# Setting the causal mask for the score maxima with GpSimd in SBUF, in place of mask products of TensorE, from the third batch on

## The chip, the core and the metric

The kernel runs on one core of a Trainium2 chip, in one launch. Five engines work side by side and wait for each other by semaphores: TensorE (in profiles PE for products and PEld for its weight loads), VectorE (DVE), ScalarE (ACT), GpSimd (POOL) and SyncE (SP, here for transfers). Each takes its instructions in the order in which the program has them. TensorE writes to PSUM; GpSimd works in SBUF. The metric is device time in microseconds (us) of one execution.

## The reference: what is computed

A block of a transformer on 8 sequences ("batches") of 256 tokens with 256 features: layer norm, attention with 32 query heads and 8 key heads of size 8, layer norm and residual, then a mixture of 8 experts (two are chosen per token) with shared experts beside them, layer norm and residual. The part that the change touches is the softmax of the attention:

```python
scores = jnp.einsum('bkgtd,bksd->bkgts', qg, k) / jnp.sqrt(jnp.asarray(hd, x.dtype))
causal = jnp.tril(jnp.ones((T, T), dtype=bool))
scores = jnp.where(causal[None, None, None, :, :], scores, jnp.asarray(-jnp.inf, x.dtype))
attn = jax.nn.softmax(scores, axis=-1)
ctx = jnp.einsum('bkgts,bksd->bkgtd', attn, v)
```

## The kernel before

**Two passes over the scores.** A batch's 256 queries are two tiles of 128 (`tt` or `t` is 0 or 1), and so are its keys. In a first pass (`maxima_of`, `maxima`, L448 to L490) TensorE forms scores with queries on the partitions, and VectorE takes each query's maximum over the keys (L484). The causal mask belongs into these scores, since a key that is not seen may not raise the maximum: on the diagonal tile a second product of TensorE (L477) adds -1e30 to what is masked, by an identity matrix times a mask in bf16. `split_shift` (L492) splits the negated maxima into two parts, `shiftT` (L499) transposes them on TensorE (`pm`), and SyncE's queue copies them as additional rows into the queries `qA` (L514). In the second pass (`weights_of`, L519) TensorE forms the scores again with keys on the partitions (`scT`, L522), now less their maxima by these rows; ScalarE takes the exponential (L530); on the diagonal tile GpSimd sets what is masked to zero in SBUF (L532). `values` (L543) multiplies by the values, into `av`; when a query tile is done, `av` is copied to `avs` (L559, by ScalarE for batches 0 and 1 and by VectorE from batch 2 on), and `softmaxed` (L562) transposes `avs` on TensorE into `pav` (L570) and divides (L574, L577).

The sweep of the first pass over a batch is cut into tiles of up to 512 columns[...]: 10 tiles for `tt` = 0 (8 of 3 key heads by 128 keys and 2 of 512 columns) and 16 tiles for `tt` = 1 (512 columns, with one or two products each), so 26 reductions, 32 score products and 32 mask products a batch. Of the mask products 8 have 384 columns, 16 have 256 and 8 have 128.

**Buffers.** Scores of both passes, the expert products `gu` and the down products `po` share five PSUM buffers (`ps_mm`, L113). Transposes, projections and the router's products share two (`ps_tp`, L114). The exponentials have nine buffers `ex` in SBUF (L1052).

**What else a batch does.** `norm1` and `normed1`, `transposed` (L324), `project` (L340: queries, keys and values, rotated by VectorE with `ra` and `rb`, summed to `full` by GpSimd, L372), `split` (L377: seven pieces a tile, each a copy and a subtraction on GpSimd, L396 and L397), `keysT` (L402, with copies `kA` by VectorE, L421 and L423), `queriesT` (L434, copies by ScalarE), the projection of the context and its norm (L610 on, `rstd` on GpSimd, L282 and L283), `residual` on GpSimd (L624), the router (`logits` L659, `first_choice` L686, `second_choice` L695, `places` L715, `shares` L708 with `den`), and `scatter` (L741): for each of two token tiles and each of two experts GpSimd multiplies a weight (L746) and issues an indirect transfer to `slots` (L752). Shared experts (`shared_gate_up` L800, `shared_down` L818) are spread between, with `th` on ScalarE (L812) and `th`, `sact` on VectorE (L813, L814).

**What sets the order.** Each step is entered by `at(when, step, ...)` (L297) with a time in units of a batch; the steps are sorted by it (L1192) and their instructions issued in that order, so that every engine's queue has them in this order. Batch b's first pass starts at b - 0.98 with 0.032 from tile to tile (L1089 to L1095), its second pass at b (L1098), its router at some b + 1.5 and its two scatters at b + 1.63 and b + 1.66 (L1140). So at any time the first pass of one batch, the second pass of the one before and the router of the one before that are in work. After the last batch come the experts' blocks (from L1195), which the change doesn't touch.

Of the kernel before, what the change touches and what calls it, by code (L numbers as in the profile page):

```python
# [10 lines left out]
F32 = mybir.dt.float32  # L11
F32R = mybir.dt.float32r
BF16 = mybir.dt.bfloat16
I32 = mybir.dt.int32
AF = mybir.ActivationFunctionType
ALU = mybir.AluOpType
# [3 lines left out]
P = 128  # L20
EPS = 1e-5
NEG = -1e30
HD = 8
HB = 32
SHIFT = 96
SQ = 32
EB = 256
# [3 lines left out]
def attn_moe_kernel(  # L31
# [46 lines left out]
    nc = tc.nc  # L78
    B, T, D = x.shape
# [10 lines left out]
    ISC = IS // P  # L90
    G = 4
    NKV = NH // G
    NK = NKV * HD
    NC = NKV // G
    J = 3
    NS = -(-NKV // J)
# [5 lines left out]
    RW = 4  # L102
# [23 lines left out]
    NREG = -(-NSLOT // (16 * EB)) * 16  # L126
# [84 lines left out]
    def set_up_router():  # L211
        nonlocal order, ones, before, upto, region0, fills, blocks, cum, unused

        order = const.tile([P, NSEL], F32, name="order")
        for e in range(NSEL):
            nc.gpsimd.memset(order[:, e : e + 1], float(NSEL - e))


        ones = const.tile([P, P], BF16, name="ones")
        before = const.tile([P, P], BF16, name="before")  # L220
        nc.gpsimd.memset(ones, 1.0)
        nc.gpsimd.affine_select(
            out=before,
            in_=ones,
            pattern=[[1, P]],
            compare_op=ALU.is_gt,
            fill=0.0,
            base=0,
            channel_multiplier=-1,
        )  # L230
        upto = const.tile([P, 2 * NSEL, 2 * NSEL], F32, name="upto")
        nc.gpsimd.memset(upto, 1.0)
        nc.gpsimd.affine_select(
            out=upto,
            in_=upto,
            pattern=[[1, 2 * NSEL], [-1, 2 * NSEL]],
            compare_op=ALU.is_ge,
            fill=0.0,
            base=0,
            channel_multiplier=0,  # L240
        )

        def counter(name, *pattern, base=0):
            sizes = [n for _, n in pattern]
            i = const.tile([P, *sizes], I32, name=f"{name}_i")
            nc.gpsimd.iota(i, pattern=[*map(list, pattern)], base=base, channel_multiplier=0)
            f = const.tile([P, *sizes], F32, name=name)
            nc.vector.tensor_copy(f, i)
            return f

        region0 = counter("region0", (NTOK, NSEL))

        fills = counter("fills", (-P, 2), (EB, NTOK // EB - 1), base=EB + P)
        blocks = counter("blocks", (1, NBLK - NSEL))
        cum = const.tile([P, NT + 1, NSEL], BF16, name="cum")
        nc.vector.memset(cum[:, 0, :], 0.0)


        unused = aconst.tile([NREG, EB, RW], I32, name="unused")
        nc.gpsimd.memset(unused, 0)  # L260
        nc.gpsimd.iota(
            unused[:, :, 1], pattern=[[1, EB]], base=NTOK, channel_multiplier=0
        )
        nc.gpsimd.memset(records, 0)
        nc.gpsimd.iota(
            records[:, :, :, 0], pattern=[[P, NT], [0, 2]], base=0, channel_multiplier=1
        )
        nc.gpsimd.iota(
            records[:, :, :, 1], pattern=[[1, NT], [0, 2]], base=0, channel_multiplier=NT
        )  # L270
# [26 lines left out]
    def at(when, step, *args):  # L297
        timeline.append((when, len(timeline), step, args))
# [100 lines left out]
    def heads_in(c):  # L399
        return min(J, NKV - c * J)  # L400
# [46 lines left out]

    def maxima_of(b, tt):  # L448

        width = (tt + 1) * P  # L450
        for c in range(NS):
            per = min(512 // width, heads_in(c))
            for k0 in range(0, heads_in(c), per):
                nk = min(per, heads_in(c) - k0)
                ng = 512 // (nk * width)
                for g0 in range(0, G, ng):
                    yield c, c * J + k0, nk, g0, ng

    def maxima(b, tt, c, k0, nk, g0, ng):

        qA, kst = qAs[b % 3], ksts[b % 3]
        if ("nmx", b, tt) not in held:
            held["nmx", b, tt] = small.tile(
                [P, NKV, G], F32, tag="nmx", name=f"nmx{b}_{tt}", bufs=2
            )
        nmx = held["nmx", b, tt]
        width = (tt + 1) * P
        sc = ps_mm.tile([P, ng, nk, width], F32, tag="mm", name="sc")
        for g in range(ng):
            nc.tensor.matmul(  # L470
                sc[:, g, :, :],
                lhsT=qA[0:SHIFT, c * G + g0 + g, ts(tt, P)],
                rhs=kst[0:SHIFT, k0 : k0 + nk, 0:width],
                start=True,
                stop=False,
            )
            nc.tensor.matmul(  # L477
                sc[:, g, :, width - P :],
                lhsT=ident_b,
                rhs=mask.unsqueeze(1).to_broadcast([P, nk, P]),  # L480
                start=False,
                stop=True,
            )
        nc.vector.tensor_reduce(  # L484
            nmx[:, k0 : k0 + nk, g0 : g0 + ng].rearrange("p k g -> p g k"),
            sc,
            AX.X,
            ALU.max,
            negate=True,
        )  # L490

    def split_shift(b, tt):  # L492
        nmx = held.pop(("nmx", b, tt))
        nhl = small.tile([P, NKV, 2, G], F32R, tag="nhl", name=f"nhl{b}_{tt}", bufs=2)
        nc.vector.tensor_copy(nhl[:, :, 1, :], nmx)
        nc.vector.tensor_tensor(nhl[:, :, 0, :], nmx, nhl[:, :, 1, :], ALU.subtract)
        held["nhl", b, tt] = nhl
# [551 lines left out]
        )  # L1049


    EX = 9  # L1052
    at(0.6, clear_slots)
    at(0.7, clear_sums)
    for i in range(PIECES):
# [18 lines left out]
    for b in range(B):  # L1074
        if b > 0:

            at(b - 2.08, norm1, b)
            at(b - 2.035, normed1, b)
            for tt in range(TT):
                a = b - 1.95 + 0.45 * tt  # L1080
                at(a, transposed, b, tt)
                at(a + 0.05, project, b, tt)
                for i in range(1 + 2 * NS):
                    at(a + 0.09 + 0.03 * i, split, b, tt, i)
                at(a + 0.22, keysT, b, tt)
                for c in range(NS):
                    at(a + 0.28 + 0.06 * c, queriesT, b, tt, c)
            at(b - 1.25, keys_apart, b)
        when = b - 0.98  # L1089
        for tt in range(TT):  # L1090
            for m in maxima_of(b, tt):
                at(when, maxima, b, tt, *m)
                when += 0.032
            at(when + 0.001, split_shift, b, tt)
            at(when + 0.07, shiftT, b, tt)  # L1095
        last = b == B - 1
        parts_of = [(c, t) for c in range(NC) for t in range(TT)]
        when, unit = b, 0.98 / (NC * 3 * G)  # L1098
        if b == 0:
            parts_of.sort(key=lambda part: part[1])  # L1100
            when, unit = -0.4, 0.04
        for c, t in parts_of:
            if b == 0 and t > 0:
                when = max(when, 0)
            for s in range(t + 1):
                for j in range(G):
                    at(when, weights_of, b, c * G + j, s, t)
                    when += unit
                at(when + 0.05, values, b, c, s, t)
            a = when + (0.1 if last else 0.12)  # L1110
            at(a, softmaxed, b, c, t)
            if c == NC - 1:
                at(a + 0.05, contextT, b, t)
                at(a + 0.09, projected, b, t)
        a = b + (1.175 if last else 1.24)
        at(a if last else a - 0.04, norm_y, b)
        at(a, normed_y, b)
        for t in range(TT):
            at(a + 0.02 + 0.01 * t, residual, b, t)
        at(a + 0.07, norm2, b)  # L1120
        at(a + (0.07 if last else 0.125), normed2, b)
        if last:
            for t in range(TT):
                at(a + 0.145 + 0.015 * t, tokensT, b, t)
            at(a + 0.175, logits, b)
            at(a + 0.1751, first_choice, b)
            at(a + 0.1752, second_choice, b)
            at(a + 0.225, places, b)
            at(a + 0.2251, shares, b)
            for t in range(TT):  # L1130
                at(a + 0.226, scatter, b, t)
            continue
        for t in range(TT):
            at(a + 0.19 + 0.02 * t, tokensT, b, t)
        at(a + 0.24, logits, b)
        at(a + 0.27, first_choice, b)
        at(a + 0.302, second_choice, b)
        at(a + 0.37, places, b)
        at(a + 0.375, shares, b)
        for t in range(TT):  # L1140
            at(a + 0.39 + 0.03 * t, scatter, b, t)
# [189 lines left out]
```

## Time and profile before

| | us |
|---|---|
| median of the runs (826.61 to 831.75) | 826.7 |
| the profiled execution: own time | 836.61 |
| the profiled execution: span, mean clock 0.962 | 834.9 |
| masks, L477: 256 products, recorded busy time | 74.6 |
| score products of the first pass, L470: 256 | 101.4 |
| reductions, L484: 208 | 129.3 |
| exponentials, L530: 192 | 113.6 |
| GpSimd's selects on the exponentials, L532: 128 | 81.3 |

The profile is of one execution, which had its own time; sums are made against that one. The page gives each engine's busy time, the same in 40 slices (a digit is tenths), the chain that ended last and the costliest groups; the trace answers for single stretches: busy times, waits ("who waited for whom") and the instructions in order of time, with start and duration. Recorded durations of TensorE's products overlap from one to the next. In the timeline lines the columns are start, duration, engine, line, operation, output and inputs, shapes, count, and in brackets the idle time before it with what ended it.

The attention takes the first 500 us, the experts' blocks the rest. The reductions of the first pass run from 92.8 to 134.6 us for batch 2, from 206.9 to 259.4 for batch 4, from 269.0 to 321.5 for batch 5, and end at 437.9 with batch 7.

### The profile page before, as it was taken

The page shows a single profiled execution, that of the slowest core. Times are in us where ns is not written, and L with a number is a line of the kernel's source. Part 1 is how long each engine was busy: PE and PEld are TensorE (multiplying, and loading weights), DVE is VectorE, ACT ScalarE, POOL GpSimd, SP SyncE. Part 2 cuts the span into 40 slices and gives each one's busy share as a digit, 9 for nine tenths or more (in the row PEclk, how much of TensorE's full clock was granted, in tenths as well). Part 3 has the DMA queues.
Part 4 walks back from the last instruction along what each step waited for, and adds up shares of the span by engine and source line. Part 5 has one row for each costly group of instructions (what it writes and reads, how often), then busy time and mean ns, then how long its engine had stood idle before and what let it go on. Part 6 is the DMA issues. An engine that isn't in the chain of part 4 may idle for free. (4 is left out here: it accounts for less than half of the span.)

```text
span 834.9 us, 11892 instructions
## 1 busy us (share of the span) xinstructions
PE 768.9 (92%) x3981; PEld 584.0 (70%) x3981; DVE 492.5 (59%) x1412; ACT 251.5 (30%) x552; POOL 345.2 (41%) x616
## 2 busy tenths in 40 slices
PE   5989899999999999999999996879999999999962
PEld 3545566766766767767666665768888888888951
DVE  5756677667677677676675546156564556532215
ACT  2554444234234244244234321011111111111203
POOL 4567455435435435435243422422222343452213
PEclk8799899999999999999999998889999999999986
DMA  5033200000000000000000005513646657578942
GB/s 152 4 85 88 87 16 16 7 22 15 7 22 15 7 21 15 8 22 15 21 8 3 20 6 202 171 40 121 213 138 186 212 160 226 174 216 302 312 117 101
DMA packets 31907, 74.62 MB, mean 89 GB/s; under 512 B 9136, under 2 KB 26032, under 8 KB 28896
## 3 DMA queue, kind: packets, MB, share of 16 engines
q1 hardware_dynamic: 20304, 58.17, 20.1%
q0 software_dynamic: 8224, 10.03, 6.2%
q10 hardware_dynamic: 3312, 5.60, 2.3%
q8 instruction: 34, 0.56, 0.3%
q14 instruction: 33, 0.27, 0.1%
HBM read 59.36 MB, written 11.80 MB: 85 GB/s over the span
## 5 line engine op out<-in xcount | busy, mean ns | idle before, releaser
L778 PE MATMUL gu<-xgT,w 128*128 128x256 f32 (+1 forms) x840 | 166.5, 358 | 6.1 <-ACT xgT L972 5.8
L778 PEld LDWEIGHTS gu<-xgT,w 128*128 128x128 f32 x840 | 146.2, 193 | 24.0 <-ACT xgT L972 6.1
L778 PE MATMUL gu<-x2T,ws_sb 128*128 128x256 f32 x640 | 156.5, 392 | 6.2 <-PEq L1232 6.1
L530 ACT ACTIVATE ex<-scT 128x512 f32<-128x512 f32 x192 | 113.6, 597 | 136.8 <-PE scT L522 123.3
L484 DVE TENSOR_REDUCE nmx<-sc 128x2 f32<-128x512 f32 (+2 forms) x208 | 129.3, 642 | 26.5 <-PE sc L477 26.2
L778 PEld LDWEIGHTS gu<-x2T,ws_sb 128*128 128x128 f32 x640 | 122.2, 197 | 28.7 <-issue 7.3
L532 POOL TENSOR_SCALAR_AFFINE_SELECT ex<-ex 128x512 f32<-128x512 f32 x128 | 81.3, 641 | 113.9 <-ACT ex L530 113.7
L1008 POOL DMA_INDIRECT sums<-yb,of x37 | 58.3, 1577 | 121.4 <-DVE yb L1007 81.3
L470 PE MATMUL sc<-kst,qA 96*128 96x512 f32 (+2 forms) x256 | 101.4, 427 | 0.7 <-issue 0.4
L522 PE MATMUL scT<-qA,kst 102*128 102x512 f32 x192 | 97.3, 515 | 1.8 <-DMA qA<-nm 1.8
L997 ACT ACTIVATE sg<-gu 128x256 f32<-128x256 f32 (+1 forms) x105 | 37.7, 359 | 196.4 <-PE gu L778 154.4
L985 DVE STREAM_TRANSPOSE xgT<-xg 32x128 f32<-32x128 f32 x240 | 72.6, 303 | 26.9 <-DMA xg<-rows,of 17.2
L791 PE MATMUL po<-w,act 128*128 128x256 f32 x370 | 83.1, 379 | 0.0
L791 PE MATMUL po<-ws_sb,sact 128*128 128x256 f32 x320 | 75.4, 393 | 5.6 <-DVE sact L814 4.2
L998 DVE TENSOR_TENSOR act<-sg,gu 128x256 f32<-128x256 f32 (+1 forms) x105 | 39.2, 387 | 63.6 <-ACT sg L997 58.7
L791 PEld LDWEIGHTS po<-w,act 128*128 128x128 f32 x370 | 69.8, 190 | 9.2
L791 PEld LDWEIGHTS po<-ws_sb,sact 128*128 128x128 f32 x320 | 61.8, 197 | 19.8 <-DVE sact L814 4.6
L477 PE MATMUL sc<-mask,ident_b 128*128 128x256 bf16 (+2 forms) x256 | 74.6, 294 | 0.0
L813 DVE SCALAR_TENSOR_TENSOR th<-th,gu 128x256 f32<-128x256 f32 x70 | 29.3, 418 | 66.3 <-ACT th L812 63.1
L926 POOL DMA_INDIRECT xg<-rows,of x39 | 37.8, 970 | 62.3 <-DMA of<-slots 29.9
L470 PEld LDWEIGHTS sc<-kst,qA 96*128 96x128 f32 x256 | 51.6, 202 | 13.6 <-issue 3.8
L550 PE MATMUL av<-ex,v_aug 128*32 128x512 f32 x384 | 58.2, 605 | 1.3 <-POOL ex L532 1.3
(167 smaller groups left out, 848.2 us busy)
## 6 DMA issues: line engine op xcount, KB each, us to landing
w<-in_routed SPq DMA_DIRECT2D x23, 1920.0 KB
ws_sb<-in_shared ACTq DMA_DIRECT2D x8, 480.0 KB
xs<-in_x SPq DMA_DIRECT2D x8, 256.0 KB
rows<-x2n SPq DMA_DIRECT2D x8, 256.0 KB
acc<-sums SPq DMA_DIRECT2D x4, 512.0 KB
sums<-ya SPq DMA_DIRECT2D x14, 128.0 KB
kst<-kA SPq DMA_DIRECT2D x16, 96.0 KB
out<-acc SPq DMA_DIRECT2D x3, 512.0 KB
```

The source lines that it names most:

```text
L470: nc.tensor.matmul(sc[:, g, :, :], lhsT=qA[0:SHIFT, c * G + g0 + g, ts(tt, P)], rhs=kst[0:SHIFT, k0 : k0 + nk, 0:width], start=True, stop= ...
L477: nc.tensor.matmul(sc[:, g, :, width - P :], lhsT=ident_b, rhs=mask.unsqueeze(1).to_broadcast([P, nk, P]), start=False, stop=True,)
L484: nc.vector.tensor_reduce(nmx[:, k0 : k0 + nk, g0 : g0 + ng].rearrange("p k g -> p g k"), sc, AX.X, ALU.max, negate=True,)
L522: nc.tensor.matmul(sc, lhsT=ksts[b % 3][0:KR, kv, ts(s, P)], rhs=qAs[b % 3][0:KR, ts(kv // J, G), ts(t, P)], start=True, stop=True,)
L530: nc.scalar.activation(e, sc, AF.Exp, scale=QSCALE)
L532: nc.gpsimd.affine_select(out=e, in_=e, pattern=[[0, G], [1, P]], compare_op=ALU.is_ge, fill=0.0, base=0, channel_multiplier=-1,)
L550: nc.tensor.matmul(av[32 * j : 32 * j + 32, :], lhsT=v_aug[b % 3 * TT + s][:, c * G + j, :], rhs=e.rearrange("p g t -> p (g t)"), start=(s ...
L778: nc.tensor.matmul(gu[:, half, :], lhsT=m[:, k, ts(i, P)], rhs=xT[:, k, :], start=(k == 0), stop=(k == KC - 1),)
L791: nc.tensor.matmul(po, lhsT=act[:, k, ts(t, P)], rhs=d[:, k, :], start=(k == 0), stop=(k == ic - 1),)
L985: nc.vector.transpose(to[ts(j, SQ), :, :, ts(i, SQ)], of[ts(i, SQ), :, :, ts(j, SQ)])
L998: nc.vector.tensor_tensor(act[:, i, :], sg, gu[:, 1, :], ALU.mult)
L1008: put = nc.gpsimd.indirect_dma_start(out=sums, out_offset=bass.IndirectOffsetOnAxis(ap=of[:, t, 1:2], axis=0), in_=y, in_offset=None, comp ...
```

## The change

The sweep over a batch's keys is cut by key tile (`kt`) as well: 10 or 12 tiles for each pair of a query tile and a key tile, of 3 heads by 128 keys (384 columns), or of the last two heads with one query group (256) or two (512). Only the diagonal tiles (`kt` = `tt`) get a mask. In batches 0 and 1 TensorE's mask product adds it as before. From batch 2 on (`BY_POOL`), ScalarE copies the diagonal scores from PSUM to one of three SBUF buffers `sm`, GpSimd sets what is masked to -1e30 there (`masked`), and VectorE reduces from `sm`. The select is entered 0.022 of a batch after its scores and the reduction 0.05 after them; the tiles follow each other in 0.026 (batches 0 and 1) or 0.024. Off the diagonal (`kt` < `tt`) VectorE reduces from PSUM with no mask. Each key tile has maxima of its own, and `split_shift` takes the smaller of the negated ones. The table `unused`, which had a buffer of its own, lies in the buffer of `sact` now.

```diff
--- before.py
+++ after.py
@@ -256,7 +256,9 @@
         nc.vector.memset(cum[:, 0, :], 0.0)
 
 
-        unused = aconst.tile([NREG, EB, RW], I32, name="unused")
+        unused = shared_pool.tile([P, ISC, T], F32, tag="sact", name="unused")
+        unused = unused[0:NREG].rearrange("p i t -> p (i t)")[:, 0 : EB * RW].bitcast(I32)
+        unused = unused.rearrange("p (r c) -> p r c", c=RW)
         nc.gpsimd.memset(unused, 0)
         nc.gpsimd.iota(
             unused[:, :, 1], pattern=[[1, EB]], base=NTOK, channel_multiplier=0
@@ -447,50 +449,75 @@
 
     def maxima_of(b, tt):
 
-        width = (tt + 1) * P
-        for c in range(NS):
-            per = min(512 // width, heads_in(c))
-            for k0 in range(0, heads_in(c), per):
-                nk = min(per, heads_in(c) - k0)
-                ng = 512 // (nk * width)
+
+        for kt in range(tt + 1):
+            for c in range(NS):
+                nk = heads_in(c)
+                ng = 1 if kt == tt and b >= BY_POOL else 512 // (nk * P)
                 for g0 in range(0, G, ng):
-                    yield c, c * J + k0, nk, g0, ng
-
-    def maxima(b, tt, c, k0, nk, g0, ng):
+                    yield kt, c, g0, ng
+
+    def scores(b, tt, kt, c, g0, ng):
+
 
         qA, kst = qAs[b % 3], ksts[b % 3]
-        if ("nmx", b, tt) not in held:
-            held["nmx", b, tt] = small.tile(
-                [P, NKV, G], F32, tag="nmx", name=f"nmx{b}_{tt}", bufs=2
-            )
-        nmx = held["nmx", b, tt]
-        width = (tt + 1) * P
-        sc = ps_mm.tile([P, ng, nk, width], F32, tag="mm", name="sc")
+        nk = heads_in(c)
+        sc = ps_mm.tile([P, ng, nk, P], F32, tag="mm", name="sc")
+        by_array = kt == tt and b < BY_POOL
         for g in range(ng):
             nc.tensor.matmul(
                 sc[:, g, :, :],
                 lhsT=qA[0:SHIFT, c * G + g0 + g, ts(tt, P)],
-                rhs=kst[0:SHIFT, k0 : k0 + nk, 0:width],
+                rhs=kst[0:SHIFT, c * J : c * J + nk, ts(kt, P)],
                 start=True,
-                stop=False,
-            )
-            nc.tensor.matmul(
-                sc[:, g, :, width - P :],
-                lhsT=ident_b,
-                rhs=mask.unsqueeze(1).to_broadcast([P, nk, P]),
-                start=False,
-                stop=True,
-            )
+                stop=not by_array,
+            )
+            if by_array:
+                nc.tensor.matmul(
+                    sc[:, g, :, :],
+                    lhsT=ident_b,
+                    rhs=mask.unsqueeze(1).to_broadcast([P, nk, P]),
+                    start=False,
+                    stop=True,
+                )
+        if kt == tt and not by_array:
+            sm = work.tile([P, ng, nk, P], F32, tag="sm", name="sm", bufs=SM)
+            nc.scalar.copy(sm, sc)
+            sc = sm
+        held["sc", b, tt, kt, c, g0] = sc
+
+    def masked(b, tt, kt, c, g0, ng):
+        sm = held["sc", b, tt, kt, c, g0]
+        nc.gpsimd.affine_select(
+            out=sm,
+            in_=sm,
+            pattern=[[0, ng * heads_in(c)], [-1, P]],
+            compare_op=ALU.is_ge,
+            fill=NEG,
+            base=0,
+            channel_multiplier=1,
+        )
+
+    def maxima(b, tt, kt, c, g0, ng):
+
+        if ("nmx", b, tt) not in held:
+            held["nmx", b, tt] = small.tile(
+                [P, tt + 1, NKV, G], F32, tag=f"nmx{tt}", name=f"nmx{b}_{tt}", bufs=2
+            )
+        nmx = held["nmx", b, tt]
         nc.vector.tensor_reduce(
-            nmx[:, k0 : k0 + nk, g0 : g0 + ng].rearrange("p k g -> p g k"),
-            sc,
+            nmx[:, kt, c * J : c * J + heads_in(c), g0 : g0 + ng].rearrange("p k g -> p g k"),
+            held.pop(("sc", b, tt, kt, c, g0)),
             AX.X,
             ALU.max,
             negate=True,
         )
 
     def split_shift(b, tt):
-        nmx = held.pop(("nmx", b, tt))
+        both = held.pop(("nmx", b, tt))
+        nmx = both[:, 0]
+        for kt in range(tt):
+            nc.vector.tensor_tensor(nmx, nmx, both[:, kt + 1], ALU.min)
         nhl = small.tile([P, NKV, 2, G], F32R, tag="nhl", name=f"nhl{b}_{tt}", bufs=2)
         nc.vector.tensor_copy(nhl[:, :, 1, :], nmx)
         nc.vector.tensor_tensor(nhl[:, :, 0, :], nmx, nhl[:, :, 1, :], ALU.subtract)
@@ -1049,7 +1076,7 @@
         )
 
 
-    EX = 9
+    EX, SM, BY_POOL = 9, 3, 2
     at(0.6, clear_slots)
     at(0.7, clear_sums)
     for i in range(PIECES):
@@ -1089,8 +1116,14 @@
         when = b - 0.98
         for tt in range(TT):
             for m in maxima_of(b, tt):
-                at(when, maxima, b, tt, *m)
-                when += 0.032
+                at(when, scores, b, tt, *m)
+                delay = 0
+                if m[0] == tt and b >= BY_POOL:
+                    at(when + 0.022, masked, b, tt, *m)
+                    delay = 0.05
+                at(when + delay, maxima, b, tt, *m)
+                when += 0.026 if b < BY_POOL else 0.024
+            when += delay
             at(when + 0.001, split_shift, b, tt)
             at(when + 0.07, shiftT, b, tt)
         last = b == B - 1
```

## Prediction

> **What bounds the kernel now.** I read the page's head and slices first, then the busy times of one stretch, then the waits of TensorE, and last the timelines of four engines around one moment of a batch.
>
> ```profile
> span 834.9 us, 11892 instructions
> PE 768.9 (92%) x3981; PEld 584.0 (70%) x3981; DVE 492.5 (59%) x1412; ACT 251.5 (30%) x552; POOL 345.2 (41%) x616
> PE   5989899999999999999999996879999999999962
> ```
> ```profile
> 206.00:268.00 62.00, 60.84 (x344) 43.71 (x344) 43.01 (x121) 22.84 (x50) 29.17 (x62) 1.00 0.05 15
> ```
>
> TensorE is nine tenths busy in nearly every slice. The second fence is one batch of the attention part (its period is 62 us: the scatters to the slots start at 188.7, 251.0, 313.1 and 375.2); the columns are PE, PE weight loads, DVE, ACT, POOL, clock, DMA. TensorE works 60.8 of 62 us at full clock, VectorE 43.0, ScalarE 22.8, GpSimd 29.2. From 190 to 400 us the only wait of TensorE that the waits view lists is 3.0 us in three places. So TensorE sets the time here, and work taken from it counts in full as long as nothing new makes it wait.
>
> **What is removed: the mask products.** A product's recorded duration overlaps the next one's, so I price a mask by the distance from its start to the start of the next, independent product:
>
> ```profile
> 269.82 0.34 PE L477 MATMUL sc<-mask,ident_b 128*128 128x384 bf16 x1
> 269.99 0.38 PE L778 MATMUL gu<-x2T,ws_sb 128*128 128x256 f32 x1
> ...
> 287.97 0.28 PE L477 MATMUL sc<-mask,ident_b 128*128 128x256 bf16 x1
> 288.09 0.38 PE L791 MATMUL po<-ws_sb,sact 128*128 128x256 f32 x1
> ...
> 298.95 0.23 PE L477 MATMUL sc<-mask,ident_b 128*128 128x128 bf16 x1
> 299.02 0.39 PE L328 MATMUL pxn<-ident,xn 128*128 128x128 f32 x2
> ```
>
> That is 0.17, 0.12 and 0.07 us for 384, 256 and 128 columns. A batch has 8, 16 and 8 of them: 1.36 + 1.92 + 0.56 = 3.84 us, and six batches lose them: **23.0 us**. By recorded durations (0.34, 0.28, 0.23) it would be 9.0 us a batch, too much. The Trainium skill, "TensorE: Matmul & The Clock Gate", section "Back-to-back issue gap", says that a warm product is spaced by its columns over 2.4 GHz plus 2.5 ns: 0.163, 0.109 and 0.056 us, 3.5 a batch and 21 us in all, an estimate. I take the trace's 23. The score products keep their columns; splitting the keys by tile makes 36 of 32 a batch, which at some 0.01 us of fixed cost each is nothing. The first two batches keep masks of the same columns: nothing.
>
> **What is added.** Per masked batch, 16 tiles of 384 and 8 of 256 columns go through ScalarE, GpSimd and VectorE.
>
> ScalarE copies: between its rows for 256 columns (0.37) and for 512 (0.58) lies 0.475: 16 x 0.475 + 8 x 0.37 = 10.6 us. ScalarE goes from 23 to 33 of some 60 us: hidden as a sum.
>
> GpSimd selects: the rows are 641 ns for 512 columns in the same form, and 507 for one of 256 in another form.
>
> ```profile
> L532 POOL TENSOR_SCALAR_AFFINE_SELECT ex<-ex 128x512 f32<-128x512 f32 x128 | 81.3, 641 | 113.9 <-ACT ex L530 113.7
> L233 POOL TENSOR_SCALAR_AFFINE_SELECT upto<-upto 128x256 f32<-128x256 f32 x1 | 0.5, 507 | 0.1
> ```
>
> 384 columns lie between 0.48 (three quarters of 641) and 0.57 (half way); I take 0.50, and 0.40 for 256: 11.2 us. GpSimd goes from 29 to 40 of 60 us: room as a sum, but not everywhere, see below.
>
> VectorE: reductions before, 8 x 0.550 + 18 x 0.683 = 16.7 us; after, 24 x 0.550, 2 x 0.683 and 8 of 256 columns at about 0.42, with one minimum of 0.27, is 18.2: +1.5 us on 43. They now read SBUF, for which no reduction row exists; equal to PSUM or 0.1 us cheaper each, this is hidden behind TensorE. The first two batches pay +0.6.
>
> The table `unused` now shares the buffer of `sact`. Its transfer is issued at 77.2 us, the first `sact` is written at 115.6: nothing.
>
> **The new wait.** A masked tile's reduction waits on VectorE for GpSimd's select, in queue order, and every third ScalarE copy (three `sm` buffers) waits for that reduction. The order of the built program shows the dangerous place: in the second half of the sweep over a batch's keys, GpSimd's queue reads select 0, two scatters, select 1, a split, two scatters, select 2, and so on. The scatters wait for the router's weights (`den`). In the trace before, one batch:
>
> ```profile
> 250.01 0.17 DVE L712 RECIPROCAL den<-den 128x2 f32<-128x2 f32 x1
> ...
> 252.66 0.68 DVE L559 COPY avs<-av 128x512 f32<-128x512 f32 x1
> ```
> ```profile
> 250.25 0.19 POOL L746 TENSOR_TENSOR records<-m,den 128x1 f32<-128x1 f32 x1 [0.85 <-DVE den L712]
> ...
> 253.54 0.28 POOL L396 CAST qs<-full 128x96 fp32r<-128x96 f32 x1
> ...
> 256.21 0.97 POOL L752 DMA_INDIRECT slots<-records,to  x1 [0.28 <-issue]
> 257.19 0.28 POOL L396 CAST qs<-full 128x96 fp32r<-128x96 f32 x1
> ```
> ```profile
> 254.33 0.60 PE L570 MATMUL pav<-ident,avs 128*128 128x128 f32 x4
> ```
>
> VectorE works without a gap from 239.0 to 253.3, so `den` comes at 250.2 in the new order too (the same three reductions lie ahead of it). The four scatters and one split then hold GpSimd from 250.25 to 257.19, and every line of that is measured. Put the selects in: select 1 ends at 254.0, the second pair of scatters at 257.7, select 2 at 258.2. Behind them in VectorE's queue stand reductions 1 and 2 (0.55 each) and then the copy `avs`, which so ends at 258.2 + 0.55 + 0.68 = 259.4 in place of 253.3. The next products on TensorE that need it, `pav`, started at 254.33, or at 253.7 with this stretch's masks gone. So TensorE waits **some 5.7 us a batch**, in order, with all else queued behind. Part of it shows as a wait for score buffers: copy 4 waits for reduction 1, and the exponentials queue behind that copy on ScalarE. Behind `avs` comes the copy of `kA`, for which the next transposes wait; I leave that out, some 0.5 us. Five sweeps meet this in full; in the first of the six, `avs` is copied by ScalarE behind copy 4 alone, about 2 us. Sum: 5 x 5.7 + 2 = **31 us** lost.
>
> In the first half of a sweep the selects meet the `full` sum, two `rstd` and the residuals on GpSimd, each waiting for VectorE. I walk this to between 0 and 1 us a batch, and take 0.5: **3 us**.
>
> **The clock.** A TensorE that stands still for long is slowed. The row:
>
> ```profile
> 500.90:503.50 2.60, 0.05 (x1) 0.08 (x2) 1.39 (x6) 0.38 (x1) 0.93 (x2) 1.00 0.00 0
> 504.40:511.20 6.80, 6.80 (x20) 5.80 (x21) 3.68 (x19) 0.71 (x3) 0.00 (x0) 0.50 0.99 359
> ```
>
> A gap of 2.55 us is followed by 6.8 us at half clock, 3.4 us of work lost. The same page of the skill, section "HAM oscillation — how this bites in real kernels", puts the rule as "no PE-idle gaps >~3.4µs". By my walk the wait comes in two pieces, about 1.5 us (score buffers) and 3 to 4 us (`pav`): by the rule few batches would trip it (0 us), by the row all six (20 us). I take 8, as part of a slow stretch hides behind other waits.
>
> **The sum.** Against the profiled execution's own 836.6 us: 836.6 - 23 + 31 + 3 + 8 = 855.6. The median of the runs is 826.7, 9.9 below that execution, so **846 us**.
>
> **The rivals.**
> - *The wait does not reach TensorE* (faster, chance 0.25). One mechanism: GpSimd is through select 2 before TensorE comes to `pav`, because scatters and selects cost its queue less than their rows, or `den` comes earlier once VectorE is relieved. It decides where the wait is 3.8 us a batch, that is where `avs` ends at 257.5; below that the change gains. For it: the sums of all engines leave 18 us or more of 60 idle; against it: the seven measured microseconds from 250.25 to 257.19 stand ahead in the same queue. With no wait: 836.6 - 23 - 9.9 = 804, with 1 us a batch 810.
> - *A draw* (0.15). The wait is 3 to 4.5 us in the five sweeps, without a slower clock: 836.6 - 23 + 16 to 27 - 9.9 = 820 to 831.
> - *The clock falls in every batch* (a part of my own case): 836.6 - 23 + 34 + 20 - 9.9 = 858; with GpSimd's selects at 0.57 and half a microsecond for `kA`, 864.
> - *GpSimd's selects are held up by VectorE.* The 128 selects of the trace, at very different loads of VectorE, average 641 ns, and those around 229 and 265 us are 0.64 and 0.65; nothing speaks for it. At 10% longer selects GpSimd would be 1.1 us later a batch, in the same place: within the range.
> - *The change does nothing.* The program's order shows 192 mask products fewer and 144 selects more; excluded.
>
> **How the numbers follow.** My case, 0.60, runs from 838 (no clock loss) to 864; a draw 0.15, faster 0.25. About 1% is what a measurement of this kernel can tell from no change, so over 835 is slower and under 818.4 faster. The range that leaves out at most 2 in 10 reaches into the faster case: 808 to 864; the likeliest case's own is 838 to 864. Faster 0.25, same 0.15, slower 0.60.
>
> **What would show it.** Right: in the profile after, TensorE waits once a batch for the copy `avs` or for a score buffer, GpSimd's selects 1 and 2 stand behind scatters, VectorE's reductions wait for GpSimd, the granted clock falls below 1.00 between 130 and 470 us, and the period grows from 62 to some 65 us. Wrong: TensorE's waits in that stretch stay near 1 us a batch and the period falls to 58. Of the saving itself: if the period shortens by less than 3.8 us with no wait added, the masks were cheaper than their spacing. If the second half of a sweep is clean and the first half is not, my walk put the wait in the wrong place.

## The result and the profile after

The changed kernel takes 872.6 us (median of four runs, 870.4 to 874.0); the kernel before takes 827.0 beside it. The ratio is 1.053 (95% interval 1.049 to 1.057): 43.5 us slower, where 19 us slower was forecast (846 us, at most 864). Ratios leave disturbed runs out, so they can differ by a few us from the quotient of two medians; below, every "+x us" is what a ratio puts on 827 us. A trace is of one execution, which can lie some us off its kernel's median (before by 9.9, mostly in the experts' part behind the attention).

The page of the kernel after, its head, TensorE's slices and the granted clock in the same slices:

```profile
span 872.2 us, 12042 instructions
PE 771.0 (88%) x3805; PEld 591.5 (68%) x3805; DVE 498.5 (57%) x1476; ACT 298.3 (34%) x696; POOL 408.1 (47%) x760
PE   5989797997997997997996999699999999999952
PEclk8899697998998998998998999889999999999977
```

The row of nines has a notch about every third slice, and the clock falls with it. One batch by the windows view (length, PE, PE weight loads, DVE, ACT, POOL, clock, DMA), and the 6.8 us behind one notch:

```profile
221.70:290.40 68.70, 60.85 (x316) 44.45 (x316) 44.21 (x131) 31.08 (x73) 39.58 (x86) 0.95 0.05 14
...
272.60:279.40 6.80, 4.86 (x15) 3.87 (x16) 4.34 (x11) 2.90 (x6) 4.96 (x14) 0.50 0.17 39
```

A batch takes 68.7 us and not 62 (forecast 65). TensorE is as busy as before, 60.9 us, though its 32 masks are gone: what they freed went into 6.8 us at half clock. GpSimd has 39.6 of 68.7 us, far from full. Its queue in that batch, VectorE behind it, and what TensorE waits for there:

```profile
265.76 1.08 POOL L779 DMA_INDIRECT slots<-records,to  x1 [0.52 <-POOL records L773]
...
267.35 0.97 POOL L779 DMA_INDIRECT slots<-records,to  x1 [0.28 <-POOL records L773]
268.33 0.53 POOL L491 TENSOR_SCALAR_AFFINE_SELECT sm<-sm 128x384 f32<-128x384 f32 x1
...
271.47 0.97 POOL L779 DMA_INDIRECT slots<-records,to  x1 [0.28 <-POOL records L773]
272.46 0.53 POOL L491 TENSOR_SCALAR_AFFINE_SELECT sm<-sm 128x384 f32<-128x384 f32 x1
```
```profile
273.02 0.55 DVE L508 TENSOR_REDUCE nmx<-sm 128x3 f32<-128x384 f32 x1 [3.57 <-POOL sm L491]
273.49 0.68 DVE L586 COPY avs<-av 128x512 f32<-128x512 f32 x1
```
```profile
270.07 0.94 PE L468 MATMUL sc<-kst,qA 96*128 96x384 f32 x2 [1.64 <-ACT sm L485]
274.23 1.12 PE L597 MATMUL pav<-ident,avs 128*128 128x128 f32 x4 [3.21 <-DVE avs L586]
```

Selects 1 and 2 stand behind two scatters each; behind select 2 stands one of VectorE's reductions, which waits 3.57 us for it, and behind that the copy `avs`; TensorE waits 1.64 us for a score buffer and 3.21 us for `avs`. That is the walk of the prediction, in its place and order. In the other sweeps the waits for `sm` and `avs` are 2.24 and 2.03 us (the first sweep, both for `sm`), 1.42 and 3.21, 3.13 alone, 3.21 alone, and 3.33 and 2.52 us.

To see where the rest comes from, the stretch of six sweeps (from the second product `pm` of one batch to that of the next, six times) is split for each kernel's trace into TensorE's idle time (length less PE's busy time in the windows view), clock time lost (length of a slow stretch times one minus its clock) and the rest, which is work at full clock:

| six sweeps, us | length | idle | clock lost | rest |
|---|---|---|---|---|
| before | 352.7 | 9.9 | 3.4 | 339.4 |
| new grouping, masks on TensorE (e1) | 359.8 | 19.0 | 1.7 | 339.1 |
| new grouping, no mask (e4) | 354.8 | 26.4 | 6.8 | 321.6 |
| the same with copies to SBUF (e3) | 359.5 | 26.8 | 8.5 | 324.2 |
| after | 402.8 | 49.9 | 32.4 | 320.4 |
| after, scatters set apart (e9) | 364.5 | 30.2 | 10.2 | 324.1 |
| after, filler in the wait (e6) | 398.4 | 35.9 | 18.8 | 343.8 |
| before, no mask (e7) | 342.7 | 21.5 | 1.7 | 319.5 |
| before, second choice twice (e15) | 361.6 | 14.4 | 6.8 | 340.4 |

Two limits of the table: idle time inside a slow stretch counts in both columns (8.9 us in the kernel after, at most 1.3 in the others), so its rest is some 4 us too low. And the ends of the stretch cut the shared experts' products differently: it holds 424 of `gu` in e1, 432 in the kernel before, e4 and e7, 440 in e3, e6, e9 and after, at 0.24 us each.

### The profile page after: what moved, and what is told of

Its sections match the earlier page's. It is cut to its first block, busy times and chain, and to the rows that moved or that the text cites. A ratio compares the mean times of both kernels' runs of the same rounds, so it can differ in the third digit from the quotient of the medians.

```text
span 872.2 us, 12042 instructions
## 1 busy us (share of the span) xinstructions
PE 771.0 (88%) x3805; PEld 591.5 (68%) x3805; DVE 498.5 (57%) x1476; ACT 298.3 (34%) x696; POOL 408.1 (47%) x760
## 4 chain that ended last, share of the span: by engine, by line
PE 62%; DVE 13%; POOL 12%; DMA 5%; issue 5%; ACT 3%; POOLq 0%; ACTq 0%; DVEq 0%; SPq 0%
PE gu L805 28%; PE po L818 15%; DMA sums<-yb,of 4%; PE av L577 4%; PE sc L468 3%; PE scT L549 3%; POOL slots L779 3%; POOL sm L491 2%; PE pqT L441 2%; DVE nmx L508 2%; PE py L624 2%; POOL ex L559 2%; PE pq L347 1%; DVE st L279 1%; DVE sact L841 1%
## 5 line engine op out<-in xcount | busy, mean ns | idle before, releaser
L805 PE MATMUL gu<-x2T,ws_sb 128*128 128x256 f32 x640 | 167.6, 412 | 9.0 <-issue 8.8
L805 PE MATMUL gu<-xgT,w 128*128 128x256 f32 (+1 forms) x840 | 163.9, 354 | 1.0 <-ACT xgT L999 0.7
L805 PEld LDWEIGHTS gu<-x2T,ws_sb 128*128 128x128 f32 x640 | 130.1, 209 | 36.3 <-issue 15.8
L468 PE MATMUL sc<-kst,qA 96*128 96x384 f32 (+1 forms) x288 | 104.5, 408 | 11.8 <-ACT sm L485 8.6
L508 DVE TENSOR_REDUCE nmx<-sm 128x3 f32<-128x384 f32 (+1 forms) x144 | 69.4, 501 | 52.7 <-POOL sm L491 52.7
L485 ACT COPY sm<-sc 128x384 f32<-128x384 f32 (+1 forms) x144 | 64.0, 447 | 91.7 <-DVE nmx L508 65.2
L549 PE MATMUL scT<-qA,kst 102*128 102x512 f32 x192 | 91.2, 489 | 2.7 <-ACT sm L485 2.0
L468 PEld LDWEIGHTS sc<-kst,qA 96*128 96x128 f32 x288 | 57.6, 207 | 37.9 <-ACT sm L485 14.5
L491 POOL TENSOR_SCALAR_AFFINE_SELECT sm<-sm 128x384 f32<-128x384 f32 (+1 forms) x144 | 68.7, 485 | 25.1 <-ACT sm L485 24.9
L818 PEld LDWEIGHTS po<-ws_sb,sact 128*128 128x128 f32 x320 | 61.8, 197 | 18.8 <-DVE sact L841 4.6
L1025 DVE TENSOR_TENSOR act<-sg,gu 128x256 f32<-128x256 f32 (+1 forms) x105 | 38.9, 387 | 60.2 <-ACT sg L1024 59.6
L508 DVE TENSOR_REDUCE nmx<-sc 128x3 f32<-128x384 f32 (+1 forms) x120 | 65.8, 578 | 10.4 <-PE sc L468 5.5
```

The lines of the kernel that those rows point to most:

```text
L468: nc.tensor.matmul(sc[:, g, :, :], lhsT=qA[0:SHIFT, c * G + g0 + g, ts(tt, P)], rhs=kst[0:SHIFT, c * J : c * J + nk, ts(kt, P)], start=Tru ...
L485: nc.scalar.copy(sm, sc)
L491: nc.gpsimd.affine_select(out=sm, in_=sm, pattern=[[0, ng * heads_in(c)], [-1, P]], compare_op=ALU.is_ge, fill=NEG, base=0, channel_multip ...
L508: nc.vector.tensor_reduce(nmx[:, kt, c * J : c * J + heads_in(c), g0 : g0 + ng].rearrange("p k g -> p g k"), held.pop(("sc", b, tt, kt, c, ...
L549: nc.tensor.matmul(sc, lhsT=ksts[b % 3][0:KR, kv, ts(s, P)], rhs=qAs[b % 3][0:KR, ts(kv // J, G), ts(t, P)], start=True, stop=True,)
L805: nc.tensor.matmul(gu[:, half, :], lhsT=m[:, k, ts(i, P)], rhs=xT[:, k, :], start=(k == 0), stop=(k == KC - 1),)
```

## The experiments

My theory after the traces: GpSimd's four scatters and one split, some 7 us in one piece, hold up the selects behind them, and everything else follows in order. Rivals: the new grouping of the score tiles; ScalarE's copies and the ring of three `sm` buffers; the number of selects.

**The change taken apart: e1, e3, e4.** Three kernels made from the changed one:

```diff
 # e1: TensorE's mask products in every batch
-    EX, SM, BY_POOL = 9, 3, 2
+    EX, SM, BY_POOL = 9, 3, 8
 # e3: no select on the scores
-                    at(when + 0.022, masked, b, tt, *m)
 # e4: neither select nor copy, maxima from PSUM
-            sm = work.tile([P, ng, nk, P], F32, tag="sm", name="sm", bufs=SM)
-            nc.scalar.copy(sm, sc)
-            sc = sm
...
-                    at(when + 0.022, masked, b, tt, *m)
-                    delay = 0.05
+                    delay = 0
```

> The changed kernel with the mask products of TensorE kept in every batch: of the change only the split of a batch's score tiles by key tile (36 groups for 32), the shared buffer of the table and the ring of sm buffers, unused here, are left. My theory (the cost is the queue at GpSimd): about 827 us, 823 to 831, as the kernel before. Rival (the regrouping itself costs): it would stay near 870. If between, the difference to 827 is the regrouping's share.

> From the third batch on neither a mask nor a copy: the maxima are reduced from PSUM over all keys of the diagonal tile, so the mask is left out of the maxima there. It measures what the removed products alone are worth. My theory: 827 - 23 = 804 us, 800 to 809, half a microsecond apart from the run without selects or up to 10 less. Rival (a mask product costs its recorded duration, 9.0 us a batch): 773 to 785. Rival (the products hid behind other waits): 815 to 827.

> The changed kernel without GpSimd's selects on the scores: ScalarE's copies to SBUF and VectorE's reductions from there stay, and the maximum is taken over all keys of the diagonal tile, so the mask is left out of the maxima (a softmax doesn't change by its shift). My theory (the select's place behind the scatters is what costs): the waits go, 806 to 815 us: 804 with no wait plus what the copies delay. Rival (ring of three sm buffers and the copies): 850 to 873. Rival (VectorE slower from SBUF): above 820.

Between e1 and e4 two small things change beside the masks: two-head diagonal tiles of 512 columns become two of 256, which is four more reductions a batch, and the tiles follow each other a little faster.

Measured: e1 834.6 us, ratio 1.0072 (1.0052 to 1.0092), +6.0 us. e4 827.7 us, 0.9969 (0.9935 to 1.0004), -2.6 us. e3 829.4 us, 1.0018 (0.9995 to 1.0042), +1.5 us. So, in steps: the grouping costs 6.0 us (I had expected at most 4), the missing masks give 8.5 (by the intervals 5 to 12), the copies cost 4 (1 to 7), and the selects cost the other 42. The selects, where they stand, are the loss; but neither kernel came near what it had expected of them (800 to 809 and 806 to 815 us). The table tells why: from the second to the third line the work falls by 17.5 us (19.4 for equal numbers of `gu`), and 7.4 us of idle time and 5.1 of lost clock come back. Where most of a batch's idle time lies, the windows view of e4 shows (one batch, and ten microseconds of it):

```profile
202.40:263.80 61.40, 57.58 (x320) 42.88 (x317) 43.46 (x130) 22.71 (x49) 29.28 (x62) 1.00 0.06 15
...
243.00:253.00 10.00, 7.59 (x41) 5.03 (x40) 9.41 (x33) 3.07 (x6) 5.75 (x11) 1.00 0.00 0
```

TensorE idles 3.8 us in this batch, 2.4 of them in these ten, where VectorE is at 9.41 of 10. Its waits there are for `rb`, whose PSUM buffer `pav` takes (1.45 us), for a score buffer (0.57) and for the router's choice (0.29).

**The scatters moved: e2 and e9.** e2 moves all four behind the last select of the sweep; e9 sets each apart (its `scatter` takes the expert as an argument).

```diff
 # e2
-            at(a + 0.39 + 0.03 * t, scatter, b, t)
+            at(a + 0.655 + 0.03 * t, scatter, b, t)
 # e9
+            for k in range(2):
+                at(a + 0.56 + 0.16 * t + 0.08 * k, scatter, b, t, (k,))
```

> The changed kernel with the scatters of the router moved behind the last select of the sweep in GpSimd's queue (due 0.265 of a batch later); nothing else. My theory: the two waits of TensorE in the second half of a sweep (1.64 and 3.21 us) and the 6.8 us at half clock behind them go, some 8 us in each of five sweeps: 872.6 - 5 x (4.9 + 3.4) = 831, and 815 to 838 with what the first halves of the sweeps still lose. Rival (ring of three sm buffers, or ScalarE's copies): the wait stays, 865 to 873. Rival (VectorE and GpSimd hold each other up): selects stay slow and the time stays above 850.

Measured: 868.9 us, 1.0471 (1.0388 to 1.0554), +39 us. By its number alone my theory had fallen. The trace of e2, GpSimd's queue and TensorE's wait, shows why:

```profile
280.68 0.97 POOL L779 DMA_INDIRECT slots<-records,to  x1 [0.28 <-POOL records L773]
281.67 1.24 POOL L559 TENSOR_SCALAR_AFFINE_SELECT ex<-ex 128x512 f32<-128x512 f32 x2
```
```profile
282.37 1.77 PE L577 MATMUL av<-ex,v_aug 128*32 128x512 f32 x2 [2.81 <-POOL ex L559]
```

The wait for `avs` in this batch is gone, and one of 2.8 us for the selects of the exponentials has taken its place: the scatters in one piece now stand ahead of those. Moving the block did not test the theory, breaking it up does:

> The changed kernel with the four scatters of a batch set apart in GpSimd's queue, one at a time behind the last selects of the sweep, with one to three selects between any two (in the run that moved all four together, TensorE's 2.8 us wait went to the selects of the exponentials behind them). My theory (about 7 us of scatters in one piece hold up whatever select is behind them, in order): no select waits more than 1.6 us for scatters, the gaps above 2 us in the second halves go and the half clock with them: 829 (as without selects) to 848. Rival (GpSimd's selects cost by their sheer number, or by the ring of three buffers, wherever the scatters are): 860 to 873.

Measured: 833.7 us, 1.0079 (1.0050 to 1.0108), +6.5 us. With the same copies, selects, scatters and ring of three, 37 of the 43.5 us are gone. In its trace a select has a single scatter ahead of it, and in this batch `pav` starts without a wait (a line without brackets had none):

```profile
255.87 1.08 POOL L779 DMA_INDIRECT slots<-records,to  x1 [0.29 <-POOL records L773]
256.97 0.42 POOL L491 TENSOR_SCALAR_AFFINE_SELECT sm<-sm 128x256 f32<-128x256 f32 x1
```
```profile
252.27 0.60 PE L597 MATMUL pav<-ident,avs 128*128 128x128 f32 x4
```

The rivals of the ring and of the number of selects fall with it: e9 is 5 us above e3, which has no select.

**The clock: e6.** Seven products of 256 columns are put into the wait for `avs`, once a batch; the transposes overwrite them.

```diff
+        if c == 1 and t == 0 and 1 <= b <= 6:
+            for _ in range(7):
+                nc.tensor.matmul(
+                    pt.rearrange("p g j r -> p (g j r)")[:, 0:256],
...
```

> The changed kernel with seven extra products of 256 columns on TensorE ahead of the first pav of the second tile's wait, once a batch in the sweeps three to eight; their result is overwritten. They fill about 3 us of the 3.2 us in which TensorE waits for avs there. Theory (a wait of that length lowers the clock to half for 6.8 us, 3.4 us of work lost each time): the dips behind this wait go, 5 to 6 times 3.4 us: 872.6 - 17 to 20 = 853 to 857, if the fillers cost nothing in the wait. Rival (the clock falls by the shorter wait ahead of it or by the load): the dips stay and the fillers come on top, 873 to 890.

Measured: 862.0 us, 1.0408 (1.0361 to 1.0455), 9.8 us less than after. The wait ahead of the fillers stayed, they take 3.2 us, and the wait behind them is 0.2:

```profile
267.16 0.94 PE L468 MATMUL sc<-kst,qA 96*128 96x384 f32 x2 [1.64 <-ACT sm L485]
267.93 3.19 PE L598 MATMUL pav<-ws_sb 128*128 128x256 f32 x14
271.31 0.66 PE L606 MATMUL pav<-ident,avs 128*128 128x128 f32 x4 [0.20 <-DVE avs L586]
```

The dips behind the wait for `avs` went. In the sweeps two to five the kernel after loses 13.6 us of clock time, e6 3.4: two dips of 3.4 us, from 201.6 us on behind a wait of 1.41 us for a score buffer and from 392.8 on behind one of 1.58 us for `rb`. Between them the clock stays at full speed:

```profile
205.00:392.00 187.00, 173.40 (x937) 127.95 (x935) 124.99 (x368) 88.17 (x208) 106.63 (x233) 1.00 0.05 15
```

So the wait for `avs` made most of the dips; after the shorter waits that stayed a dip came in two of the four sweeps. But a batch became shorter by 1.6 us (68.7 to 67.1) and not by 3.4: the fillers add some 4 us of work where the idle time falls by 2.4, and `kA`, behind `avs` on VectorE, is waited for 0.96 instead of 0.31 us. What a dip costs net this run does not settle, since it brought work of its own.

**What the masks were worth: e7, e10, e12, e11.** e7 is the kernel before without mask products in any batch. e10 is e4, e12 the kernel before and e11 is e7, each with one more line changed:

```diff
-            copier(b)(avs, held.pop(("av", b, c, t)))
+            nc.scalar.copy(avs, held.pop(("av", b, c, t)))
```

> The kernel before, its score tiles grouped as they were, without the mask products in any batch: the maxima are taken over all keys of the diagonal tile, so the mask is left out of them. The run without masks in the new grouping gave only 7 us against its twin with masks: TensorE's busy time fell by 3.3 us a batch, but 1 to 1.5 us of idle came with it, and its grouping had cost 6 to 7 already. Theory of the prediction (the masks' time counts in full): 800 us and below. Theory now (VectorE works without a gap for 14 us of each batch and sets the pace there, so that only a part of the masks' time is gained): 812 to 820. Rival (the masks' time is not gained at all): 825 to 829.

> As the run with neither mask nor copy from the third batch on (the mask is left out of the maxima there), and the copy avs, four of 0.68 us a batch, made by ScalarE in every batch instead of VectorE from the third. Theory now (VectorE's gapless 14 us set the pace of that stretch): 1.4 us a batch come off that stretch, and TensorE's idle time falls from 3.8 to about 2.4 us a batch: 827.65 - 6 x 1.4 = 819, 814 to 822. Rival (TensorE's waits there come of something other than VectorE's load): 825 to 830. Rival (ScalarE, in order, becomes late): above 830.

> The kernel before with the copy avs made by ScalarE in every batch; masks stay. It takes four times 0.68 us a batch off VectorE, 1.36 us of it out of the stretch without a gap. Theory now (VectorE and TensorE both close to setting the pace): TensorE idles only 1.16 us a batch, so at most that comes back, 0 to 1 us a batch: 823 to 829. Rival (TensorE alone sets the pace): 828 to 830. Rival (ScalarE becomes late): above 831.

> The kernel before without mask products (the mask is left out of the maxima, which are taken over all keys of the diagonal tile), and with the copy avs made by ScalarE in every batch. Theory now (what TensorE lost by the masks is held back by VectorE): both edits together give more than the two apart: TensorE's busy time is 57.5 us a batch, its idle falls from 2.7 to 1.5 or 2: 822.8 - 6 x 0.7 to 1.2 = 815 to 819. Rival (avs has nothing to do with it): 822 to 824.

| | us | ratio (interval) | us to before |
|---|---|---|---|
| e7 | 822.8 | 0.9913 (0.9885 to 0.9940) | -7.2 |
| e10 | 823.4 | 0.9941 (0.9921 to 0.9961) | -4.9 |
| e12 | 825.7 | 0.9967 (0.9950 to 0.9985) | -2.7 |
| e11 | 815.9 | 0.9862 (0.9835 to 0.9890) | -11.4 |

In the old grouping, with nothing put in their place, the 256 masks of all eight batches are worth 7.2 us. In e7 a steady batch has 57.5 us of work in place of 61.0, and 2.5 to 2.9 us of idle time in place of 1.2; it falls from 62.1 to 60.2 us. The first lines of e7's waits view for 139 to 440 us (waiter, what it waited for, us in total, times, longest):

```profile
PE pav L563 <- DVE rb L364: 4.0, 4, 1.0
PE place L715 <- DVE chosen L692: 2.0, 5, 1.0
PE pqT L439 <- DVE kA L423: 1.9, 7, 0.4
PE pqT L439 <- POOL qs L397: 1.5, 3, 0.9
```

In all, TensorE waits there 10.0 us for VectorE, 2.6 for ScalarE and 1.5 for GpSimd; in the kernel before it is 5.3, 0.2 and 0. Relief of VectorE in the stretch brings the kernel before 2.7 us. For the kernel without masks (e10 against e4) it is 2.3 us, which the intervals don't tell from nothing, and less than I had expected (the 1.4 us wait for `rb` stayed). e11 gives 1.5 us more than e7 and e12 together, which is inside their intervals: that the two edits help each other is not shown. e11 is faster than both kernels of this case.

**VectorE loaded: e15.** The kernel before, with one more line:

```diff
+        best(held["s", g], 2)
         m2, hot2 = best(held.pop(("s", g)), 2)
```

> The kernel before, with the five small operations of VectorE that find the second choice made twice (the first result isn't used): about 1.04 us more on VectorE a batch, in the middle of the 14 us in which it works without a gap; nothing is added on TensorE, masks stay. Theory now (VectorE sets the pace of that stretch already in the kernel before): TensorE's wait for rb, 0.99 us a batch, grows to about 2 us, 0.8 to 1.04 us a batch in eight batches: 829 + 6 to 8 = 835 to 837. Rival (TensorE sets the pace everywhere, as the prediction took it): 829 to 831.

Measured: 837.2 us, 1.0116 (1.0096 to 1.0136), +9.6 us, for about 7 us of work (0.9 a batch in its trace, where I had put 1.04) on an engine that is busy 59% of the time. TensorE in one batch:

```profile
245.15 0.17 PE L723 MATMUL place<-chosen,before 128*128 128x8 bf16 x1 [0.71 <-DVE chosen L700]
...
246.50 0.63 PE L570 MATMUL pav<-ident,avs 128*128 128x128 f32 x4 [0.99 <-DVE rb L364]
```

The wait shows at `chosen`, not at `rb` as I had written; with the old one close behind it, it brought a dip of 3.4 us at half clock in three of the four batches that have both. By the table, 4.5 us of the loss is idle time and 3.4 lost clock. So work added to VectorE in that stretch costs TensorE time already in the kernel before.

**The router later: e14.** e11 with the router's second choice behind `ra` and `rb`:

```diff
-        at(a + 0.302, second_choice, b)
-        at(a + 0.37, places, b)
-        at(a + 0.375, shares, b)
+        at(a + 0.32, second_choice, b)
+        at(a + 0.40, places, b)
+        at(a + 0.405, shares, b)
...
-            at(a + 0.39 + 0.03 * t, scatter, b, t)
+            at(a + 0.42 + 0.03 * t, scatter, b, t)
```

> As the run without mask products and with avs on ScalarE (the mask is left out of the maxima), and the router's second choice, its places, shares and scatters put 0.02 to 0.03 of a batch later, behind the two products ra and rb on VectorE and behind pav and two score products on TensorE. TensorE waited 1 to 1.4 us a batch for rb, which frees the PSUM buffer that pav takes. Theory: that wait goes or becomes a shorter one for chosen, 0.5 to 1.4 us a batch: 3 to 8 us under its twin, 808 to 815. Rival (VectorE's work in the stretch must be done in any order): the wait shows up at chosen or at the next pav, within 2 us of its twin.

Measured: 826.4 us, 0.9959 (0.9937 to 0.9981), 8 us more than its twin. The wait for `rb` did go. But the scatters, moved along, now stand ahead of the splits of the queries, and TensorE waits up to 2.1 us for `qs`, 7.4 us in five places between 139 and 440 us:

```profile
260.55 0.97 POOL L745 DMA_INDIRECT slots<-records,to  x1 [0.28 <-POOL records L739]
261.52 0.28 POOL L396 CAST qs<-full 128x96 fp32r<-128x96 f32 x1
261.88 0.39 POOL L397 TENSOR_TENSOR qs<-full,qs 128x96 fp32r<-128x96 f32 x1
```

Neither side of the expectation held. By this trace the scatters in one piece are the cause once more; e14 with its scatters set apart was not run.

## Why the prediction was right or wrong

| step | forecast | measured | by |
|---|---|---|---|
| mask products gone | -23.0 | -8.5 (5 to 12) | e1 to e4; -7.2 by e7, all eight batches |
| new grouping | 0 | +6.0 | before to e1 |
| copies, reductions from SBUF | 0 | +4 (1 to 7) | e4 to e3 |
| selects: waits and clock | +42 (31 + 3 + 8) | +42 | e3 to after |
| sum | +19 | +43.5 | |

**The step that failed** is the one from the first view to the first term: "work taken from it counts in full as long as nothing new makes it wait". The price of a mask was nearly right: TensorE lost 19.9 us of work in the six sweeps of e7 against 23.0 forecast, 3.4 us in a steady batch against 3.84. (The 21 us by the skill's formula were a check only. Its section "Back-to-back issue gap" gives that formula for a product alone and says that it under-counts products of few columns in a stream; nothing rests on it.) The effect was not: 11.6 us of idle time came back in e7, and the gain was 10.0 us in the six sweeps of its trace; by the medians all eight batches together gained 7.2 us, where 23.0 were forecast for six.

TensorE's busy 60.8 of 62 us hid that its inputs come just in time in many places. One is the 14 us of each batch in which VectorE has no gap either. In the trace before, `chosen` ends at 244.53 and `place`, which needs it, starts at 244.63, with the 0.99 us for `rb` behind it; the window holds 9.0 us of TensorE and 9.3 of VectorE in ten:

```profile
241.40:251.40 10.00, 9.01 (x54) 6.05 (x53) 9.32 (x35) 3.18 (x7) 3.97 (x9) 1.00 0.01 2
```
```profile
244.36 0.17 DVE L699 TENSOR_TENSOR chosen<-hot,hot 128x16 bf16<-128x16 f32 x1
...
244.63 0.17 PE L722 MATMUL place<-chosen,before 128*128 128x8 bf16 x1
```

I had that gapless row in hand, and used it for when `den` comes, not for what it says of the saving. Masks in such a stretch are cover, and without them TensorE waits: e15 (load on VectorE costs at once) and the slice of e4 show this, where TensorE idles 1.7 to 2.4 us in the stretch, in e1 1.3 to 1.7. It is not the whole, though. Only 8 of a batch's 32 masks stand in that stretch, 0.76 us by the prediction's spacing, or 4.6 us in six batches. And of the 1.5 us by which a steady batch of e7 idles longer than before, 0.5 lie there; the others are waits of 0.2 to 0.4 us, all over the batch, for copies and splits on VectorE, ScalarE and GpSimd that the masks had covered. Which of these could be had back was not tried. Of e4's gain 5.1 us more went into a dip in its first sweep; which part of that is the kernel's and which the start's is open.

**The grouping at nothing** was the second error: I counted products. The table shows hardly more work on TensorE (339.4 and 339.1, with 8 products `gu` fewer in the second, some 2 us) but 9 us more idle time; VectorE has 43.9 in place of 43.1 us a batch, and TensorE's new waits in a steady batch are above all for `cx` and for `ex`. Which of the tiles' new order and VectorE's 0.8 us makes them was not tried apart.

**The wait** was right in place, cause and order, and e9 shows the cause. A select of 384 columns took 0.52 us (forecast 0.50), and a reduction from SBUF 0.55 as from PSUM. That its term of 42 us is met to the microsecond is luck: its two parts are wrong in opposite directions. From e3 to after the six sweeps have 23 us more idle time (forecast 34) and 24 us more lost clock (forecast 8). The waits for `avs` and `sm` come to 26.4 us (forecast 31). Here the row and the rule of the Trainium skill ("TensorE: Matmul & The Clock Gate", "HAM oscillation — how this bites in real kernels") had stood against each other: by the rule of gaps above 3.4 us nothing should be lost, by the row 20 us. The trace sides with the row: no gap of TensorE in the six sweeps is longer than 3.33 us, and yet each of the five later sweeps has one of 3.1 to 3.3 us with 3.4 to 6.8 us at half clock at its end; in the first they are 2.6 and 2.8 us, and a pair of 2.2 and 2.0. I took 8, between the two, where only the row was measured on this kernel. Not all of the lost clock is the walk's: two of the dips (from 330.6 and 398.9 us on) stand behind 1.58 us for `rb`, a wait of this length that e3 has too, without selects. What a dip costs net was not measured (e6 brought work of its own), so the split in wait and clock stays open; their sum does not.

**The first sweep** was taken for the mildest (2 + 0.5 us) and became 16.7 us longer (50.1 to 66.8), with 7.9 us more idle time and 10.2 more lost clock; the later ones grew by 6.9, 6.5, 6.3, 3.5 and 10.2. Its first half waits 2.8 us for the residual on GpSimd, which my walk had put at half a microsecond, and its second half 2.2 and 2.0 us for `sm`, where the walk had about 2 in all.

**The rivals.** *The wait does not reach TensorE* named scatters and selects in one queue as what decides, and e9 shows that they do. But the 804 us that I gave it were not reached: with the wait nearly gone, e9 is at 833.7 us. A saving of 3.8 us a batch was not there to break even with.

## What to carry to other kernels

Before a saving on the busiest engine is counted in full, look in the timeline for places where that engine finds its input ready just in time, above all beside a second engine without a gap: much of the work removed there returned as idle time here (11.6 of 19.9 us in e7). When a step is moved to an in-order queue, ask what already stands there in one piece; moving the block changed its victim (e2, e14), breaking it up took away 37 of 43.5 us (e9).

## What the runs showed of the hardware

The clock fell after shorter waits than I had expected. Single waits of TensorE of 2.5 to 3.3 us within 80 and 520 us stood at or shortly before the start of 3.4 to 13.7 us at half clock in every trace looked at. After shorter ones it came out both ways: of four waits of 1.45 us in e4 one was followed by such a dip, a wait of 2.1 us in e14 was not. In e15 0.71 and 0.99 us within two microseconds brought a dip in three of four batches, while 0.99 us alone did so in one of four batches of e1 and in none of four in the kernel before.
